# A twelve-part decoder on one core: when the split operands are made, which engine evacuates, and where masks, biases and one-hots are made

## The chip, the core and the metric

The kernel runs on one core of a Trainium2 chip. The metric is the device time of one execution in microseconds; the time of a kernel is the median of several runs. The profile is of one further execution, and its own time is given beside it. Engines are called PE (TensorE, with PEld for its weight loads), DVE (VectorE), ACT (ScalarE), POOL (GpSimd) and SP (SyncE, which only issues DMAs here).

## What is computed

A pre-norm decoder of four layers works on x, 4 batches of 256 rows of 128 numbers, in fp32. Each layer adds three things to x, each computed from a layer norm of x: a self attention, a cross attention to a context of 4 x 512 x 128, and a feed-forward part.

```python
x = x + L0_attn(norm(x))      # 16 heads of 8, with biases
x = x + L0_xattn(norm(x), ctx, key padding mask)
x = x + L0_ffn(norm(x))       # shared expert + 1 of 32 routed experts
x = x + L1_attn(norm(x))      # causal, scores clipped to +-10
x = x + L1_xattn(norm(x), ctx)        # strided keys
x = x + L1_ffn(norm(x))       # 2 of 8 experts
x = x + L2_attn(norm(x))      # linear attention
x = x + L2_xattn(ctx, mask, norm(x))  # 16 heads of 64, keys: ctx and latents
x = x + L2_ffn(norm(x))       # 2 of 8 experts, with biases
x = x + L3_attn(norm(x), causal mask) # low rank
x = x + L3_xattn(norm(x), ctx, ctx, full mask)
x = x + L3_ffn(norm(x))       # ternary weights, quantised activations
```

In an attention, `out = softmax(q k^T) v`, then `out @ Wo + bo`. The weights of one softmax sum to one, so a bias on v comes out as `bv @ Wo`, the same for every row.

## The kernel before

x stays in SBUF as eight tiles of 128 rows; batch b has tiles 2b and 2b+1. The stages follow one another: layer 0 (self and cross attention together, about 0 to 272 us of the span), its experts (to 328), layer 1's attentions (to 466) and experts (to 558), linear attention (to 631), latent attention (to 1068), its experts (to 1163), and layer 3 (to the end).

**Units and slots.** In layers 0, 1 and 3, `woven` (L432) works on units: one batch of one attention. Layers 0 and 3 have eight, four of self attention and four of cross attention (`self_units` L888 or `low_rank_units` L935, and `cross_units` L910). A unit needs a pass over its rows, which only finds each row's maximum (`rows_of` L546, read by DVE in L571 or, with an additive mask, in L575), and a pass over its columns, which makes the scores again in transposed form, less the maxima, and exponentiates them on ACT (`columns_of` L635, L673). Then `weighted` (L695, L701) multiplies with the values, and the result is divided (L719, L721), transposed, projected and added to x (L740). Slot n weaves, beat by beat, the columns of unit n with the rows of units n+1 and n+2; a beat is two groups of tiles (`beat` L756, `beats` L774). Only the last beats of a slot touch rows of unit n+2. At the end of a slot the maxima of unit n+1 are split in three bf16 parts (`parts` L599), transposed (`parts_T` L614: L629, or L620 and an addition in L626 for split units), and its columns can begin.

Everything that has to be done in a slot is a pair of a position between 0 and 1 and a function; `run` (L849) sorts them and issues them. In layers 0 and 3 this order is the order of the instructions on DVE, ACT, PE and POOL (`manual_schedule`, L857 to L859), each of which takes its own in order. `front` (L811) places the prelude of unit n+2 (norm, source, for cross units key source, then queries and keys), the values of unit n+1 (0.6), and the list `beside`; `back` (L829) places the beats and what follows them.

**Split units.** From the third unit on (`u.split`, L854), the queries and keys of layers 0 and 3 are split in three bf16 parts on POOL (`in_parts` L467, L471 to L474), written to DRAM by three DMAs each (L496, L520), and read back in the layout that the row scores need (L497, L526). All these DMAs are issued by SP, in order. Row scores are then L582, column scores L679. Three sets of buffers rotate.

**Norms.** `statistics` (L300) has its sums on DVE (L308, L309), the power on POOL (L314, L316) and the scaling (L322) on POOL where `on=G`. `turned` (L883) transposes a pair of tiles on PE (L332) and moves it out of PSUM with `evacuate` (L288), which alternates between DVE (L292) and ACT (L294).

**Between stages.** The experts' results lie in DRAM. `bring` (L1373) gathers a batch of them with indirect DMAs on POOL (L1379: two per batch after layer 0, four after layers 1 and 2), `add` (L1386) adds them to x. They are kept in `unsettled`; `settle` (L1219), called from a unit's norm, keeps two batches fetched and adds one. In the expert stages `blocks_of` (L1122) turns expert choices into blocks of rows: ranks, one-hots of ranks (L1136), block numbers, and at last `token` (L1197), which the first gather (L1284) waits for.

**Masks.** `key_mask` (L373) loads a mask and turns it into numbers on DVE (L387); the latent stage calls it at its start (L1879). `added_mask` (L2267) does it for layer 3, whose four masks are made at the stage's start (L2326, L2327). In layer 3 a mask is added to the row scores by DVE while it takes their maximum (L575) and to the column scores by a product with the identity on PE (L643).

Of the kernel before, what the change touches and what calls it, by code (L numbers as in the profile page):

```python
# [101 lines left out]
def _layout(i):  # L102
# [31 lines left out]
        _col(bq[:128][byd]), _col(bq[128:256][byd]),  # L134
# [4 lines left out]
        _col(f["L0_xattn_q_b"][byd]), _col(bk[:128][byd]),  # L139
# [13 lines left out]
        _col(f[k + "bq"][byd]), _col(f[k + "bk"][byd]),  # L153
# [50 lines left out]
def decoder(ctx: ExitStack, tc: tile.TileContext, dr, out):  # L204
# [81 lines left out]
    turn = [0]  # L286

    def evacuate(dst, src):  # L288

        turn[0] ^= 1  # L290
        if turn[0]:
            V.tensor_copy(dst, src)  # L292
        else:
            A.copy(dst, src)  # L294
# [106 lines left out]
    class Unit:  # L401
# [7 lines left out]
        def __init__(u, b, nk, weights, prelude, context, q_bias=None, k_bias=None, v_bias=None,  # L409
                     rows_mask=None, row_mask=None, cols_mask=None, key_bias=None, clip=False):  # L410
            u.b, u.nk, u.weights, u.prelude, u.context = b, nk, weights, prelude, context
            u.q_bias, u.k_bias, u.v_bias = q_bias, k_bias, v_bias
# [19 lines left out]
    def woven(pool, units, n_keys, split=None, lent=None):  # L432
# [95 lines left out]
        def values(u):  # L528
# [10 lines left out]
            if u.v_bias is None:  # L539
                V.tensor_copy(dst, src)  # L540
            else:
                bias = u.v_bias.rearrange("p (h d) -> p h d", h=H)
                for i in range(u.nkt):
                    V.tensor_tensor(dst[:, i], src[:, i], bias, ALU.add)

        def rows_of(u, qt, g, half):  # L546
# [6 lines left out]
            def made(j, r):  # L553
# [9 lines left out]
                def score(i, r=r, sc=sc):  # L563
                    T.matmul(
                        sc[:, i, :], lhsT=u.qm[r, g + i, qt * P : (qt + 1) * P], rhs=u.kc[r, :],
                        start=u.row_mask is None, stop=True,
                    )

                def read(j=j, sc=sc):
                    if u.rows_mask is None:  # L570
                        V.tensor_reduce(u.mx[:, qt, j, g : g + per], sc, AX.X, ALU.max)  # L571
                        return
# [23 lines left out]
                return [], rounds, read  # L596
# [214 lines left out]
        def front(n):  # L811
# [3 lines left out]
            if n + 2 < len(units):  # L815
                u = units[n + 2]
                if u.split:
                    end = 0.35 if units[n].nk < SK else 0.5
                    out += spread(prelude(u)[1 if n else 0 :], 0.0, end)
                else:  # L820
                    out += spread(prelude(u), 0.0, 0.95 - lead)
            if split and n + 3 < len(units):
                out += [(0.8, prelude(units[n + 3])[0])]
# [31 lines left out]
        halves_of_rows = [halved(groups_of_rows(u)) for u in units]  # L855

        by_hand = {mybir.EngineType.DVE, mybir.EngineType.Activation, mybir.EngineType.PE}  # L857
        by_hand.add(mybir.EngineType.Pool)
        with tc.manual_schedule(engines=by_hand) if split else nullcontext():  # L859
# [3 lines left out]
            if len(units) > 1:  # L863
                first += spread(prelude(units[1]), 0.0, 0.8)
            first += beats([], halves_of_rows[0] + halves_of_rows[1][:LEAD], units[0])[0]
# [10 lines left out]
            run(carried)  # L876

# [9 lines left out]

    def self_units(pool, w, biased, clip, first_row):  # L888
        q_bias = scaled(pool, w[:, 512:513]) if biased else None

        def norm(u):
            settle()
            u.xn = normalised(u.b, pool, on=G)

        def source(u):
            u.source = u.key_source = turned(u.xn, pool)
            if biased:
                add_bias(2 * u.b, first_row + 1)
                add_bias(2 * u.b + 1, first_row + 1)

        return [
# [3 lines left out]
                **dict(q_bias=q_bias, k_bias=w[:, 513:514], v_bias=row(first_row)) if biased else {},  # L905
            )
            for b in range(B)
        ]

    def cross_units(pool, w, first_row, context, **masks):  # L910
# [5 lines left out]
        def source(u):  # L916
            u.source = turned(u.xn, pool)
            add_bias(2 * u.b, first_row + 1)
            add_bias(2 * u.b + 1, first_row + 1)

        def key_source(u):
# [3 lines left out]
        return [  # L925
# [3 lines left out]
                q_bias=q_bias, k_bias=w[:, 513:514], v_bias=row(first_row),  # L929
# [3 lines left out]
        ]  # L933

    def low_rank_units(pool, w, **masks):  # L935
        up = w[:, 192:448]

        def norm(u):
            settle()
# [57 lines left out]
    class Router:  # L997
# [3 lines left out]
        def __init__(r, pool, name, n_e, k, per, gate, probs=False, scored=False, xnT=None):  # L1001
# [9 lines left out]
            r.rank = kept("rank", [P, r.n])  # L1011
            r.sent = dram.tile([NT * P, D], F32, tag=name + "sent", name="sent")

        def steps(r, pool, b, tag):
# [105 lines left out]
            return out + [ranks]  # L1120

    def blocks_of(pool, r, size, widths):  # L1122
# [5 lines left out]

        def in_block(which):

            w = small.tile([P, 16], I32, tag="wi", name="wi", bufs=1)[:, :n]
            V.tensor_scalar(w, which, P - 1, None, ALU.bitwise_and)
            wb = small.tile([P, 16], BF16, tag="wb", name="wb", bufs=1)[:, :n]
            V.tensor_copy(wb, w)
            place = pool.tile([P, n, P], BF16, tag="place", name="place", bufs=1)
            V.tensor_tensor(  # L1136
                place, iotab.unsqueeze(1).to_broadcast([P, n, P]),
                wb.unsqueeze(2).to_broadcast([P, n, P]), ALU.is_equal,
            )
            return place  # L1140
# [19 lines left out]
        if per == P:  # L1160
            ranks = small.tile([P, 16], I32, tag="ranks", name="ranks", bufs=1)[:, :n]
            V.tensor_copy(ranks, r.rank)
            place = in_block(ranks)
# [8 lines left out]
        if per < P:  # L1172
            place = in_block(index)
# [15 lines left out]
        V.tensor_scalar(block[:, 1], block[:, 1], partition, None, ALU.mult)  # L1189
        fill(3, "g")  # L1190
# [28 lines left out]
    def settle():  # L1219

        while unsettled and len(fetched) < 2:
            fetch, add = unsettled.pop(0)
            fetched.append(call(add, fetch()))
        if fetched:
            fetched.pop(0)()

    def mixture(pool, r, weights, wh, wd, activate, biases=None):
# [158 lines left out]
        def add(brought):  # L1386
            for t, i, back in brought:
                if weights is None:
# [477 lines left out]
    def latent_attention(wkv, wqo, router):  # L1866
# [9 lines left out]
        with ExitStack() as st:  # L1876
            st.enter_context(psum_pool("ps2x"))
            pool = attn_pool(st, "l2x")
            neg1, neg1T = key_mask(pool, "mbf1", True)  # L1879
# [372 lines left out]
    def normalise_context(b, i):  # L2252
        for t in (NKT * b + i, NKT * b + i + 1):
            V.tensor_scalar(
# [22 lines left out]
    def layer_0(wh, router):  # L2277
        with ExitStack() as st:
# [7 lines left out]
            def loads():  # L2286
                for i in range(0, 16, 4):
                    cols = slice(i * 512, (i + 4) * 512)
                    tc.keep_in_program_order(A.dma_start(wh[:, cols], dr["e0h"][:, cols]))

            units = self_units(pool, w0a, True, False, 0)
            units += cross_units(
# [4 lines left out]
            for u in units[:B]:  # L2297
# [88 lines left out]
```

## Time and profile before

| | us |
|---|---|
| median of 3 runs | 1498.5 (1496.29 to 1503.18) |
| the profiled execution's own time | 1496.84 |
| its span, first to last instruction | 1495.0 |
| PE, DVE, ACT, POOL busy | 1280.2, 827.9, 723.0, 324.1 |
| mean granted clock of PE | 0.915 |
| PE busy in layer 0's slots (34 to 240) | 180.5 of 206 |
| PE busy in layer 3's slots (1196 to 1435) | 216.2 of 239 |
| exponentials of columns (L673), ACT | 384 of 598 ns |
| maxima of 512 columns (L571), DVE | 192 of 684 ns |

A row of the groups names the line, engine, tile written and tiles read. A row of the waits says who waited for whom, in total, how often and at most. A row of the windows gives the stretch, its length, the busy time of PE, PEld, DVE, ACT and POOL with their instructions, then the granted clock of PE (1.00 is full speed), the DMA engines' share and GB/s. The chain goes back from the last instruction to whatever released each step; its pieces are start, length and line.

### The profile page before, as it was taken

The page shows a single profiled execution, that of the slowest core. Times are in us where ns is not written, and L with a number is a line of the kernel's source. Part 1 is how long each engine was busy: PE and PEld are TensorE (multiplying, and loading weights), DVE is VectorE, ACT ScalarE, POOL GpSimd, SP SyncE. Part 2 cuts the span into 40 slices and gives each one's busy share as a digit, 9 for nine tenths or more (in the row PEclk, how much of TensorE's full clock was granted, in tenths as well). Part 3 has the DMA queues.
Part 4 walks back from the last instruction along what each step waited for, and adds up shares of the span by engine and source line. Part 5 has one row for each costly group of instructions (what it writes and reads, how often), then busy time and mean ns, then how long its engine had stood idle before and what let it go on. Part 6 is the DMA issues. An engine that isn't in the chain of part 4 may idle for free.

```text
span 1495.0 us, 29472 instructions
## 1 busy us (share of the span) xinstructions
PE 1280.2 (86%) x11199; PEld 702.3 (47%) x11200; DVE 827.9 (55%) x2696; ACT 723.0 (48%) x1462; POOL 324.1 (22%) x481
## 2 busy tenths in 40 slices
PE   4879998796787998879999999999689389899984
PEld 2434454353354664535555565554456244444442
DVE  6568884585555446555445444543323466777743
ACT  1434667285542334357766756766212024445563
POOL 4332220344123316000000000000141542323000
PEclk8889999896897999999999999999889569999997
DMA  3531220520232116230110000000311211322000
GB/s 139 195 108 63 64 67 20 232 55 11 85 138 90 40 34 212 77 128 15 57 43 20 27 5 1 1 4 1 117 39 40 59 57 51 110 64 77 6 5 8
DMA packets 50873, 95.85 MB, mean 64 GB/s; under 512 B 6881, under 2 KB 31947, under 8 KB 49067
## 3 DMA queue, kind: packets, MB, share of 16 engines
q1 hardware_dynamic: 45742, 73.42, 14.4%
q10 hardware_dynamic: 1728, 13.86, 2.3%
q0 software_dynamic: 3264, 6.69, 2.1%
q8 instruction: 90, 1.47, 0.4%
q14 instruction: 49, 0.40, 0.1%
HBM read 66.20 MB, written 29.72 MB: 64 GB/s over the span
## 4 chain that ended last, share of the span: by engine, by line
PE 63%; DVE 12%; ACT 7%; POOL 7%; issue 5%; DMA 5%; SPq 1%; ACTq 0%; POOLq 0%; DVEq 0%
PE o L2047 6%; PE g L1306 6%; PE o L701 6%; PE s L2027 5%; PE f L1973 4%; PE s L582 4%; PE y L1330 3%; PE s L679 3%; DVE mx L571 2%; PE s L643 2%; PE f L1959 2%; PE s L364 2%; PE s L656 2%; POOL back L1379 2%; PE t L1315 2%
## 5 line engine op out<-in xcount | busy, mean ns | idle before, releaser
L673 ACT ACTIVATE pr<-s 128x512 f32<-128x512 f32 x384 | 206.1, 598 | 228.6 <-PE s L679 152.0
L314 POOL TENSOR_SCALAR ve<-mv 128x2 f32<-128x2 f32 x44 | 10.1, 230 | 739.4 <-DVE mv L309 739.2
L1984 ACT ACTIVATE ss<-ss,ntop 128x768 f32<-128x768 f32 x128 | 118.6, 928 | 91.8 <-DVE ntop L1982 91.6
L701 PE MATMUL o<-pr,v 128*32 128x256 f32 (+1 forms) x1792 | 145.8, 400 | 9.1 <-ACT os L707 5.5
L571 DVE TENSOR_REDUCE mx<-s 128x1 f32<-128x512 f32 (+1 forms) x192 | 122.5, 684 | 50.1 <-PE s L679 22.4
L1978 DVE CUSTOM_DVE_ANT_0 ss<-f,n 128x512 f32<-128x512 f32 x128 | 83.5, 688 | 69.2 <-PE f L1973 69.2
L2047 PE MATMUL o<-pr,v 128*64 128x256 f32 x768 | 109.4, 397 | 1.0 <-ACT pr L2034 0.9
L575 DVE CUSTOM_DVE_ANT_0 junk<-s,nmif 128x512 bf16<-128x512 f32 x128 | 82.8, 686 | 35.3 <-PE s L679 34.6
L2027 PE MATMUL s<-qT,kT 64*128 64x256 f32 x768 | 101.1, 382 | 0.0
L2034 ACT ACTIVATE pr<-s,n 128x512 f32<-128x512 f32 x128 | 80.3, 679 | 30.0 <-PE s L2027 29.8
L582 PE MATMUL s<-e0h 32*128 32x512 bf16 (+1 forms) x576 | 72.3, 361 | 15.8 <-DMA e0h<-kp 15.2
L1284 POOL DMA_INDIRECT xb<-sent,token x62 | 59.8, 965 | 103.5 <-PE t L1291 58.4
L1973 PE MATMUL f<-kT,qT 64*128 64x512 f32 x256 | 77.1, 629 | 2.2 <-ACT kT L294 1.1
L1966 DVE CUSTOM_DVE_ANT_0 ss<-f,nought 128x256 f32<-128x256 f32 x128 | 46.7, 421 | 54.8 <-PE f L1959 51.8
L2047 PEld LDWEIGHTS o<-pr,v 128*64 128x64 f32 x768 | 48.4, 137 | 58.6 <-issue 25.9
L701 PEld LDWEIGHTS o<-pr,v 128*32 128x32 f32 x1792 | 39.0, 110 | 71.2 <-issue 48.6
L2027 PEld LDWEIGHTS s<-qT,kT 64*128 64x128 f32 x768 | 67.8, 191 | 6.2
L679 PE MATMUL s<-e0h 32*128 32x256 bf16 x960 | 68.4, 276 | 2.5 <-DVE mx L571 1.7
L332 PE MATMUL s<-consts,xn 128*128 128x128 f32 x64 | 20.3, 369 | 54.7 <-POOL xn L322 54.7
L575 DVE CUSTOM_DVE_ANT_0 junk<-s,nmcau 128x256 bf16<-128x256 f32 x128 | 46.2, 420 | 28.1 <-PE s L656 12.0
L656 PE MATMUL s<-qm,kc 32*128 32x512 f32 (+1 forms) x256 | 60.0, 676 | 0.0
L322 POOL TENSOR_SCALAR xn<-x,mv,rs 128x128 f32<-128x128 f32 x72 | 57.7, 809 | 3.8
(482 smaller groups left out, 2643.9 us busy)
## 6 DMA issues: line engine op xcount, KB each, us to landing
qp<-qp SPq DMA_DIRECT2D x36, 192.0 KB, 2.3
kd<-ahead SPq DMA_DIRECT2D x20, 256.0 KB, 2.0
vd<-ahead SPq DMA_DIRECT2D x20, 256.0 KB
kT<-kd SPq DMA_DIRECT2D x20, 256.0 KB, 4.8
v<-vd SPq DMA_DIRECT2D x5, 1024.0 KB, 5.3
e0h<-qp SPq DMA_DIRECT2D x6, 768.0 KB
e0h<-in_e0h ACTq DMA_DIRECT2D x4, 1024.0 KB, 7.2
e0h<-in_e0h SPq DMA_DIRECT2D x1, 4096.0 KB
```

The source lines that it names most:

```text
L571: V.tensor_reduce(u.mx[:, qt, j, g : g + per], sc, AX.X, ALU.max)
L575: V.tensor_tensor_reduce(junk[:, : u.nk], sc[:, i, :], u.rows_mask(qt), 1.0, -3e38, ALU.add, ALU.max, accum_out=u.mx[:, qt, j, g + i : g + ...
L582: T.matmul(sc[:, i, :], lhsT=u.q3[r, g + i, c, qt * P : (qt + 1) * P], rhs=u.kk[r, g + i, : u.nk], start=n == 0, stop=n == 3 * per - 1,)
L656: T.matmul(sc, lhsT=u.kc[r, kt * P : (kt + 1) * P], rhs=u.qm[r, gp : gp + 2, first:], start=u.clip, stop=True,)
L673: A.activation(dst, sc, AF.Exp)
L679: T.matmul(sc[:, i, :], lhsT=u.kk[r, gp + i, kt * P : (kt + 1) * P], rhs=u.q3[r, gp + i, c, :], start=u.cols_mask is None and n == 0, stop ...
L701: T.matmul(u.po[gp][32 * j : 32 * j + 32, i, first:], lhsT=u.v[:, kt, 4 * j + gp + i, :], rhs=u.pr[gp, kt, j][:, i, first:], start=kt + i ...
L1306: T.matmul(p[r], lhsT=xbT[b][:, r], rhs=w(512 * i), start=biases is None, stop=True,)
L1973: T.matmul(sc[h], lhsT=qT[u, c][hrow[h], qt * P : (qt + 1) * P], rhs=kT[u, c][hrow[h], :SK], start=True, stop=True,)
L1984: A.activation(ss[qt][h], ss[qt][h], AF.Exp, bias=ntop[:, qt, h, c : c + 1], accum_out=total[:, qt, h, c : c + 1],)
L2027: T.matmul(sc[h][:, i, :], lhsT=kT[u, c][hrow[h], kt * P : (kt + 1) * P], rhs=qT[u, c][hrow[h], :], start=False, stop=i == 1,)
L2047: T.matmul(po[u, g][hrow[h], i, :], lhsT=v[u][:, kt, n * hd : (n + 1) * hd], rhs=pr[u, g, kt, h][:, i, :], start=kt + i == 0, stop=kt + i ...
```

## The change

- **Preludes.** For a split unit n+2, queries and keys go to 0.06 and 0.12 of slot n. What comes ahead of them is done in slot n-1: norm at 0.68, source (and key source) between 0.8 and 1.0. For the third unit the norm is at 0.85 of the opening and the source at 0.02 of slot 0.
- **`reducing`.** While layers 0 and 3 are woven, `evacuate` and the values' copy always use ACT.
- **Biases.** The value bias is multiplied with the output weights once (`output_bias`) and added to x with the output bias, by POOL, beside the unit's slot.
- **First units.** The first unit of layers 1 and 3 fetches only its own batch, adds and normalises tile by tile, with the scaling on DVE, and fetches the second batch then (`settled_LN`). The first unit of layer 3 gets its row mask by a product on PE.
- **Masks and context.** The latent stage's mask is made ahead of the linear attention. Layer 3's full masks are made beside units 1 and 2. Layer 0's context is normalised on POOL (L2254). The first half of the routed weights is loaded one quarter a slot in slots 0 to 3.
- **One-hots.** The last router makes the one-hots of ranks batch by batch; three of four are made in the latent stage.

```diff
     def evacuate(dst, src):
         turn[0] ^= 1
-        if turn[0]:
+        if turn[0] and not reducing:
             V.tensor_copy(dst, src)
         else:
             A.copy(dst, src)
...
-            if u.v_bias is None:
+            if reducing:
+                A.copy(dst, src)
+            else:
                 V.tensor_copy(dst, src)
-            else:
-                bias = u.v_bias.rearrange("p (h d) -> p h d", h=H)
-                for i in range(u.nkt):
-                    V.tensor_tensor(dst[:, i], src[:, i], bias, ALU.add)
...
+                by_product = u.rows_mask is not None and u.n == 0
+
+                def masks():
+                    T.matmul(
+                        sc, lhsT=identb,
+                        rhs=u.rows_mask(qt).unsqueeze(1).to_broadcast([P, per, u.nk]),
+                        start=True, stop=False,
+                    )
                 def read(j=j, sc=sc):
-                    if u.rows_mask is None:
+                    if u.rows_mask is None or by_product:
                         V.tensor_reduce(u.mx[:, qt, j, g : g + per], sc, AX.X, ALU.max)
                         return
...
                 if u.split:
-                    end = 0.35 if units[n].nk < SK else 0.5
-                    out += spread(prelude(u)[1 if n else 0 :], 0.0, end)
+                    steps = prelude(u)
+                    out += [(0.06, steps[-2]), (0.12, steps[-1])]
+                    if n == 0:
+                        out += [(0.02, steps[1])]
                 else:
                     out += spread(prelude(u), 0.0, 0.95 - lead)
             if split and n + 3 < len(units):
-                out += [(0.8, prelude(units[n + 3])[0])]
+                steps = prelude(units[n + 3])
+                out += [(0.68, steps[0])] + spread(steps[1:-2], 0.8, 1.0)
...
+            if split:
+                first += [(0.85, prelude(units[2])[0])]
...
+    def output_bias(pool, w, n):
+        made = []
+        def make():
+            t = pool.tile([P, S], F32, tag="q", name="q")[:, :P]
+            V.tensor_copy(t, w[:, 514:515].to_broadcast([P, P]))
+            acc = product(t, w[:, 384:512], "s1")
+            made.append(pool.tile([P, P], F32, tag=f"ob{n}", name=f"ob{n}", bufs=1))
+            V.tensor_tensor(made[0], acc, row(n), ALU.add)
+        def add(u):
+            for t in (2 * u.b, 2 * u.b + 1):
+                G.tensor_tensor(x[t], x[t], made[0], ALU.add)
+        return make, add
...
+    def to_one_hots(place, which):
+        n = which.shape[1]
+        w = small.tile([P, 16], I32, tag="wi", name="wi", bufs=2)[:, :n]
+        if which.dtype != I32:
+            V.tensor_copy(w, which)
+            which = w
+        V.tensor_scalar(w, which, P - 1, None, ALU.bitwise_and)
+        wb = small.tile([P, 16], BF16, tag="wb", name="wb", bufs=2)[:, :n]
+        V.tensor_copy(wb, w)
+        V.tensor_tensor(
+            place, iotab.unsqueeze(1).to_broadcast([P, n, P]),
+            wb.unsqueeze(2).to_broadcast([P, n, P]), ALU.is_equal,
+        )
...
-        while unsettled and len(fetched) < 2:
+        while len(fetched) < 2 and unsettled:
+            bring_next()
+        if fetched:
+            fetched.pop(0)()
+
+    def bring_next():
+        if unsettled:
             fetch, add = unsettled.pop(0)
             fetched.append(call(add, fetch()))
-        if fetched:
-            fetched.pop(0)()
+
+    def settled_LN(b, pool):
+        if not fetched:
+            bring_next()
+        add = fetched.pop(0)
+        xn = []
+        for t in (2 * b, 2 * b + 1):
+            add(t)
+            n = pool.tile([P, D], F32, tag="xn", name="xn", bufs=5)
+            normalise([x[t]], [n])
+            xn.append(n)
+        bring_next()
+        return xn
...
-            V.tensor_scalar(
+            G.tensor_scalar(
                 cn[:, t, :], cn[:, t, :], context_mv[:, t, 0:1], context_rs[:, t : t + 1],
...
-            mf, mfT = added_mask(pool, "mif1", 2, False), added_mask(pool, "mif1T", NKT, False)
...
+            units[1].beside += [make, call(full_mask, "mif1", 2)]
+            units[2].beside += [call(full_mask, "mif1T", NKT)]
...
+    with tc.tile_pool(name="late2", bufs=1, reuse_waits="tile") as late2:
+        latent_mask = key_mask(late2, "mbf1", True)
```

The hunks that only pass these things on are left out.

## The prediction, written before the result was known

> **What bounds the kernel now.** The page's shares come first, then its slices, then the chain of work that ended last, the table of waits for TensorE, and the timeline around the longest waits.
>
> ```profile
> PE 1280.2 (86%) x11199; PEld 702.3 (47%) x11200; DVE 827.9 (55%) x2696; ACT 723.0 (48%) x1462; POOL 324.1 (22%) x481
> ...
> PEclk8889999896897999999999999999889569999997
> ...
> PE 63%; DVE 12%; ACT 7%; POOL 7%; issue 5%; DMA 5%; SPq 1%; ACTq 0%; POOLq 0%; DVEq 0%
> ```
>
> TensorE is busy 86% of the span, but only 63% of the chain; the rest is handovers, and its clock sags at the start, around the middle of layer 0 and at the start of layer 3. The change leaves TensorE's work as it is, so what it can win is waits, and the slow clock after them. The waits of TensorE in layer 0 (34 to 250 us) and layer 3 (1200 to 1300 us), as "who waited for whom: us, times, longest":
>
> ```profile
> PE s L582 <- DMA e0h<-kp: 15.2, 4, 5.5
> PE s L620 <- DVE mp L612: 2.3, 3, 1.3
> PE s L650 <- DVE mT L292: 1.7, 1, 1.7
> ...
> PE s L582 <- DMA cn<-kp: 3.8, 1, 3.8
> PE s L582 <- DMA kk<-kp: 2.3, 1, 2.3
> PE s L332 <- POOL xn L322: 2.1, 2, 1.8
> ```
>
> The row scores (L582) wait six times, 21.2 us, for operands that go out to DRAM and back. One such trip in the chain of waits, unit 3 of layer 0:
>
> ```profile
> 65.15 0.48 ACT q L491
> ...
> 68.68 1.92 SPq L496
> ...
> 72.65 1.92 DMA kp<-kp
> ...
> 74.58 5.57 DMA e0h<-kp
> ...
> 80.29 0.37 PE s L582
> ```
>
> From the query copy to the first matmul it takes 15.1 us; the others 13.6 (unit 2), 14.1 (unit 4), in layer 3 12.4 and 15.0. After each wait the granted clock (third number from the end) is near a half for 5 to 7 us:
>
> ```profile
> 56.00:60.00 4.00, 4.00 (x38) 1.60 (x34) 2.01 (x6) 1.09 (x2) 0.31 (x1) 0.55 0.46 162
> 80.00:88.00 8.00, 7.71 (x69) 3.82 (x70) 2.91 (x7) 1.71 (x4) 4.37 (x7) 0.57 0.16 66
> 106.00:112.00 6.00, 5.65 (x67) 3.20 (x68) 2.96 (x7) 1.49 (x3) 2.43 (x5) 0.60 0.02 4
> 1232.00:1238.00 6.00, 6.00 (x47) 2.21 (x44) 2.01 (x12) 1.49 (x4) 2.26 (x3) 0.57 0.01 4
> ```
>
> **The change part by part**, against the profiled execution's own 1496.84 us (span 1495.0).
>
> **1. Operands a slot ahead (-16.5).** A slot lasts from one transpose of the row maxima (L629, L620) to the next: 26.0, 25.3, 25.2, 30.0, 33.7, 32.4, 33.9 us in layer 0. Unit n+2's queries and keys sit at about 0.17 and 0.29 of slot n (0.19 and 0.44 in cross slots); they go to 0.06 and 0.12. Its rows are first read after six of eight beats, 0.75 of a self slot. Without its wait and half its slow clock a self slot lasts some 20 us, so rows are wanted 15 us after its start, and the trip ends at 1.2 + 13.6 to 15.1 = 14.8 to 16.3. I leave 4.7 us of the 21.2 in place. SP's queue carries the same DMAs; the 4 MB of e0h on ScalarE's queue go out 1 MB a slot instead of all in slot 0. Ends: -21 and -5.
>
> **2. The clock after those waits (-7.5).** About 29 us run at half speed behind five of them; were TensorE alone the limit, 14.5 would go. A beat there is some 2.0 us with 2 x 684 ns of VectorE in it, so I take half. [...]
>
> **3. A new wait on the transposes (+8).** The norm moves from 0.8 to 0.68 of the slot, but the transpose (L332) that needs it moves from early in the next slot to 0.8 to 1.0 of the same one. The nearest trace of that:
>
> ```profile
> 1208.67 0.29 DVE L308 BATCH_NORM_STATS2 st<-x 128x6 f32<-128x128 f32 x1
> ...
> 1210.82 1.57 POOL L322 TENSOR_SCALAR xn<-x,mv,rs 128x128 f32<-128x128 f32 x2
> ...
> 1211.68 0.47 PE L332 MATMUL s<-consts,xn 128*128 128x128 f32 x1 [1.84 <-POOL xn L322]
> ```
>
> Statistics to xn take 3.7 us, and VectorE runs behind its place (in slot 4 the statistics of 0.8, due at 164.7, come at 167.87: 3.2 us). The room is 0.17 x 20 = 3.4 us in self slots (0.22 for a self unit: 4.4), 0.17 x 33 = 5.6 in cross ones. With a lag of 1 us in self and 2.5 in cross slots, the five slots lose 0.3 + 1.3 + 1.3 + 0.6 + 0.6 = 4.1, twice 8.2. Behind the waiting transpose stand all of TensorE's later beats. Ends: 0 and +25.
>
> **4. Less on VectorE (-6).** In a cross slot of layer 0 it loses four bias adds (4 x 283 ns, L544), four context normalisations (4 x 338, L2254) and half its evacuations (0.95): 3.4 us of 25 to 27 busy. Layer 3 loses 1.5. At each slot's end VectorE is last (chain of 165 to 172: half is L571), yet mid-slot TensorE leads. I pass on 0.4 of it in slots 3 to 6 of layer 0 (5.4) and 0.2 in layer 3's (1.2). Ends: 0 and -15. ScalarE takes the copies (about 1.5 us a slot; busy 20 of 32): covered, but not in the last slots, where only exponentials run: +1.2. GpSimd takes the 16 normalisations. [...] The folded value biases cost one product and two copies a layer: under 1 us, beside the first slots.
>
> **5. First units (-7.5).** At layer 3's start GpSimd issues eight gathers (1.25 us each) from 1163.78, and ve starts at 1173.61. With four they end at 1168.8; tile 1's sums land at 1170.2, then 0.5 statistics, 1.1 ve and rs, 0.34 on VectorE: 1172.8 instead of 1176.4. The other four gathers go where GpSimd waits for q (1176.4 to 1180.7); after qm, four more and the norm, unit 1's xn comes about 3 us sooner. Unit 2's norm in the opening removes the 1.84 + 0.30 + 0.46 at 1211.68 (2.6), mT on ScalarE rather than behind VectorE's reads 0.8 here and 1.7 at 33.8. Layer 1: two gathers more before unit 1, +0.5 (-1.5 to +1.5).
>
> **6. Masks.** The latent stage opens with VectorE idle 5.0 us for mrow (L387), then 1.4 of work; keys wait behind it and L1959 starts at 640.68. Without it, some 637, where the key loads land too: -3.5, less 0.3 if the mask's DMA is late in the stage before. In layer 3 the two full masks become 512 KB loads behind a bounce on SP, read by VectorE at 0.83 and 0.75 of slots 1 and 2; if the load is not there VectorE stands, and with it the reads that free PSUM: +2 (0 to +5). Masks by product: 16 reads of 0.61 us (L571's pace) for 32 of 0.345, -1.3 on VectorE, against 16 matmuls like L643's (0.5 us at half clock) on a TensorE 12 of 33 us busy: 0 (-1.3 to +3).
>
> **7. One-hots (-1.3).** At ffn2's start L1136's 2.29 us and three casts leave the token chain, about 1.0 of it stays. Nothing, if xb does wait for line<-part, as the chain has it.
>
> Sum: -16.5 - 7.5 + 8 - 6 + 1.2 - 7.5 - 3.2 + 2 - 1.3 = -30.8, so 1466.0; the median shown is 1.66 above the profiled time, so 1467.7: **1468**.
>
> **Rivals.**
> - **All of it works:** -21, -12, part 3 at +3, VectorE -9, rest as above: -48, **1451**. For it: TensorE has no other wait over 2 us in those slots. 0.12.
> - **The trip still decides:** a slot that shrinks also brings the need forward, and 13.6 to 15.1 us are wanted out of some 15. Part 1 gives 8, part 2 gives 2: +14, **1482**. 0.13.
> - **Nothing measurable:** part 3 eats parts 1 and 2 (+16 more, and VectorE's relief not passed on, +6, masks +3): **1493**. The change then doesn't do what it says. 0.09.
> - **Slower:** TensorE, in order, stands at L332 for GpSimd's xn. Price: 3.7 + 3.2 of lag + 0.8 for a normalisation in front, less 3.4 to 5.6 of room, 2 to 4 us, and a half-clock stretch of 3 us: 6.5 in ten slots, 65 instead of 8, **1525**. It decides from 3.9 us a slot, where the 38.8 of the other parts are gone. Against it: the lag shrinks with VectorE's load. 0.08.
> - The forecast: 0.58.
>
> **How the numbers follow.** Range 1443 to 1492: it leaves out most of the slower case and some of the best and the unmeasurable one. Faster by over 0.5% (about what a measurement can tell from no change; under 1491): 0.58 + 0.12 + 0.13 = 0.83; within: 0.09; slower: 0.08.
>
> **What would show it.** Right: L582 waits for its DMA under 6 us in all; no half-clock stretch after 60 us in layer 0's self slots; unit 0's second xn of layer 3 near 1173 less what was won before; no DVE wait on mrow. Wrong: L332 waiting for xn over 10 us in all, VectorE idle for mi in layer 3, ACT rows ending the last slots later.

## The result, and the profile after

The changed kernel takes **1475.0 us** (median of 4 runs, 1473.1 to 1481.2) beside 1498.1 for the one before (one run more than above): ratio 0.985, 95% interval 0.983 to 0.988. That is 23 us faster; 30 were forecast. The profiled execution spans 1472.6 us. Its page, in the rows that answer to those of before (engine sums, granted clock in 40 slices, the chain by engine):

```profile
PE 1267.6 (86%) x11222; PEld 698.2 (47%) x11222; DVE 810.2 (55%) x2586; ACT 738.5 (50%) x1502; POOL 335.1 (23%) x497
...
PEclk8979999896897999999999999999889679999997
...
PE 68%; DVE 12%; ACT 7%; POOL 4%; issue 4%; DMA 3%; SPq 0%; ACTq 0%; POOLq 0%; DVEq 0%
```

TensorE's share of the chain rose from 63 to 68%: DMA and GpSimd gave up five points. TensorE's waits in layer 0 (34 to 250 us), then at the start of layer 3 (1183 to 1290):

```profile
PE s L591 <- DMA e0h<-kp: 13.3, 3, 9.7
...
PE s L333 <- POOL xn L323: 2.8, 2, 2.5
```

```profile
PE s L333 <- POOL xn L323: 4.2, 2, 3.9
```

L591 (L582 before) still waits 13.3 us in layer 0, now mostly in one wait of 9.7; in layer 3 its DMA waits are gone. Among the slots, L333 (L332) waits for xn at one place in each layer, the start of slot 0.

By stage, from the same marks in both traces (transposes of maxima, first gathers, first latent row scores):

| stretch | before | after | difference | by the prediction's steps |
|---|---|---|---|---|
| start to layer 0's last slot | 237.8 | 231.4 | -6.4 | about -20 |
| to ffn0's gather, to layer 1's gather | 95.0 | 93.8 | -1.2 | 0 |
| layer 1, to ffn1's gather | 145.9 | 149.7 | +3.8 | +0.5 |
| to the linear attention; to the first latent rows | 162.0 | 157.2 | -4.8 | -3.2 |
| latent stage, to ffn2's gather | 444.6 | 437.0 | -7.6 | -1.3 |
| ffn2, to layer 3's gather | 78.5 | 78.4 | -0.1 | 0 |
| layer 3 | 331.3 | 325.2 | -6.1 | about -7.6 |

So the total is right partly by luck, because misses cancel: layer 0 gave 13 us less than forecast and layer 1 3 less, the latent stage with its opening 8 more. One profile's stretch is uncertain by up to some 4 us: three of the runs below (e0h's loads in the cross slots; the same with layer 1's gathers ahead; that with the one-hots at ffn2's start) have the same code up to layer 1, and took 95.6, 99.3 and 95.3 us for the second row. The clock differs from execution to execution: the four runs of the changed kernel were granted 0.922 to 0.931 of full speed, and the slowest had the lowest.

The 9.7 us wait, in SyncE's timeline, in the DMA engines' share (the number before the last) while SyncE stands, and in the chain of waits of the changed kernel:

```profile
62.89 1.85 SPq L521 DMA_DIRECT2D kp<-kp  x3
64.80 0.49 SPq L523 DMA_DIRECT2D kp<-n  x1
75.58 0.33 SPq L498 DMA_DIRECT2D e0h<-qp  x1
```

```profile
66.00:70.00 4.00, 4.00 (x64) 2.21 (x56) 3.16 (x8) 2.05 (x5) 1.24 (x2) 1.00 0.04 8
```

```profile
70.59 0.06 ACT pr L683
70.65 4.92 DMA e0h<-in_e0h
...
75.58 0.33 SPq L498
...
76.02 4.70 DMA e0h<-kp
...
80.85 0.37 PE s L591
```

SyncE has issued the last leg of unit 3's operands to DRAM by 65.3, but it issues the read-back (L498) only at 75.58, in the instant in which an unrelated 1 MB load of e0h, issued by ScalarE at 70.65, has landed. From 66 to 70 the DMA engines were 4% busy, so it was not their bandwidth that it lacked. The semaphores in the trace say why. The 266 DMAs of SyncE and ScalarE in it use eight, 101 to 108, 33 or 34 times each, and the next DMA in time takes the next of them in 263 of 265 steps. The other two are here: L497 at 60.50 passes over 101, and the load and L498 both take it.

```
SyncE    60.50 to 64.80  3 qp<-qp, 3 kp<-kp, 1 kp<-n  raise 102 to 108
SyncE    65.34, 65.39    (L498, unit 3)               waits for 103, for 104 and 102: three of its legs
ScalarE  70.65           e0h<-in_e0h (load of slot 1) raises 101 sixteen times, from 74.87 to 75.57
SyncE    75.58           e0h<-qp (L498, unit 3)       waits for 101, raises 101
```

The load stands ahead of the legs in the program, but ScalarE, whose order is written by hand, reaches it 10 us after SyncE began the legs (60.50).

### The profile page after: what moved, and what is told of

Its sections match the earlier page's. It is cut to its first block, busy times and chain, and to the rows that moved or that the text cites. A ratio compares the mean times of both kernels' runs of the same rounds, so it can differ in the third digit from the quotient of the medians.

```text
span 1472.6 us, 29442 instructions
## 1 busy us (share of the span) xinstructions
PE 1267.6 (86%) x11222; PEld 698.2 (47%) x11222; DVE 810.2 (55%) x2586; ACT 738.5 (50%) x1502; POOL 335.1 (23%) x497
## 4 chain that ended last, share of the span: by engine, by line
PE 68%; DVE 12%; ACT 7%; POOL 4%; issue 4%; DMA 3%; SPq 0%; ACTq 0%; POOLq 0%; DVEq 0%
PE o L711 6%; PE o L2131 6%; PE g L1388 6%; PE s L2111 5%; PE s L591 4%; PE f L2057 4%; PE s L689 3%; PE y L1412 3%; PE s L653 3%; DVE mx L580 3%; PE s L365 2%; PE s L666 2%; PE f L2043 2%; PE s L2104 2%; PE t L1397 2%
## 5 line engine op out<-in xcount | busy, mean ns | idle before, releaser
L683 ACT ACTIVATE pr<-s 128x512 f32<-128x512 f32 x384 | 206.1, 599 | 180.6 <-PE s L689 128.6
L315 POOL TENSOR_SCALAR ve<-mv 128x2 f32<-128x2 f32 (+1 forms) x46 | 10.6, 231 | 740.1 <-DVE mv L310 739.9
L580 DVE TENSOR_REDUCE mx<-s 128x1 f32<-128x512 f32 (+1 forms) x208 | 132.0, 683 | 64.8 <-PE s L689 24.5
L591 PE MATMUL s<-e0h 32*128 32x512 bf16 (+1 forms) x576 | 69.3, 350 | 13.9 <-DMA e0h<-kp 13.3
L333 PE MATMUL s<-consts,xn 128*128 128x128 f32 x64 | 20.7, 370 | 58.0 <-POOL xn L323 40.2
L666 PE MATMUL s<-qm,kc 32*128 32x512 f32 (+1 forms) x256 | 57.5, 662 | 0.0
L1461 POOL DMA_INDIRECT back<-done,index x40 | 39.6, 991 | 52.2 <-DMA done<-ys 33.8
```

Of the source, the lines that this page charges most:

```text
L591: T.matmul(sc[:, i, :], lhsT=u.q3[r, g + i, c, qt * P : (qt + 1) * P], rhs=u.kk[r, g + i, : u.nk], start=n == 0, stop=n == 3 * per - 1,)
L666: T.matmul(sc, lhsT=u.kc[r, kt * P : (kt + 1) * P], rhs=u.qm[r, gp : gp + 2, first:], start=u.clip, stop=True,)
L683: A.activation(dst, sc, AF.Exp)
```

## Experiments

Ratios, with their 95% intervals, are to the kernel before in runs on the same chip. The first four kernels ran on one chip, the next four on a second, the last four on a third; between these groups the ratios are compared, not the medians.

**Loads in slot 0 again** (1483.3 us; 0.990, 0.987 to 0.993).

```diff
-                u.beside += [call(context_scales, u.b), call(loads, u.b)]
+                u.beside += [call(context_scales, u.b)]
+            units[0].beside += [call(loads, i) for i in range(4)]
```

> The changed kernel, with the four 1 MB loads of e0h all issued in slot 0 again, instead of one per slot. Theory (turn of the semaphores): in the changed kernel's program the read-back of unit 3's queries (L498) is given the same DMA completion semaphore as the e0h load that stands eight transfers ahead of it, so it can't be issued before that load has landed; that is the 9.72 us wait at 80.85. With the loads in slot 0 they have landed by then: the L591 wait of slot 1 falls to 2 us or less, slot 1 from 29.7 to some 22 us, and the whole to 1465 to 1469. Rival (crowding): the wait comes of the loads sharing the DMA engines with the operands' legs; then moving them into slot 0 only moves it to slots 0 and 1, L591 keeps 8 us or more of waits in layer 0, and the time stays at 1473 to 1477.

Slot 1 fell from 29.7 to 21.1 us as the first theory has it, but slot 0 rose from 22.1 to 34.7 with a wait of 12.8, so the time missed both. SyncE's timeline, and ScalarE's:

```profile
42.66 12.07 SPq L521 DMA_DIRECT2D kp<-kp  x3
58.46 0.29 SPq L523 DMA_DIRECT2D kp<-n  x1
```

```profile
49.21 0.38 ACTq L2372 DMA_DIRECT2D e0h<-in_e0h  x1
...
51.01 0.33 ACTq L2372 DMA_DIRECT2D e0h<-in_e0h  x1
```

Three key legs, 1.9 us elsewhere, last 12.1, to 54.73. A load took 5.0 us to land in this run, which puts the landing of the one of 49.21 at 54.2, when the third leg begins if it is as long as elsewhere (0.55 us); and the burst of transfers that the loads are part of, from 50.0 on, is over at about 58, just ahead of L523 at 58.46. From 45.2 to 50.0 the DMA engines were 2% busy, so crowding doesn't explain the wait of the third leg in that time; the turn of the semaphores, seen in the changed kernel's trace, would explain both waits. That the third leg waits for the first load and L523 for the second is thus the author's estimate from these times. Four loads in slot 0 are not harmful in themselves: before, they were issued together, from 57.5 to 59.4, between two units' legs.

**Loads in the cross slots** (1471.7; 0.981, 0.979 to 0.983).

```diff
-                u.beside += [call(context_scales, u.b), call(loads, u.b)]
+                u.beside += [call(context_scales, u.b)]
...
                 u.beside += [call(normalise_context, u.b, i) for i in range(0, NKT, 2)]
+                u.beside += [call(loads, u.b)]
```

> The changed kernel, with the four loads of e0h one each in the cross slots 4 to 7, where no row score of the self slots waits. Both theories (turn of the semaphores, crowding) expect slot 1's wait at L591 to fall from 9.7 us to under 2 and the time to 1464 to 1469. They differ beside the run with the loads in slot 0: by the turn of the semaphores the two are within 2 us of each other, by crowding this one is 6 us or more the faster. If neither holds (SP's own order, or GpSimd's splits, decide), slot 1 stays at 28 us or more in both.

Slot 1 took 19.9 us without a DMA wait, as expected, though the time came down by only 3.3 (by the ratios 6.6, and the two intervals just overlap), less than expected: this profile lost 5 us more than the changed kernel's to the slow clock in slot 0. It was 12 us faster than the run with the loads in slot 0, which crowding had foretold in size; but by the estimate above that run's loss was the semaphores' too.

**Row masks in VectorE's reads** (1478.1; 0.987, 0.984 to 0.990).

```diff
-                by_product = u.rows_mask is not None and u.n == 0
+                by_product = False
```

> The changed kernel, with the row masks of layer 3's first unit not made by product on TensorE, but in VectorE's read of each head as before. Theory (the product lies on the path): TensorE has the 16 mask products (0.455 us each) ahead of scores that VectorE is already waiting for, so from unit 1's normalised rows to the first transpose of maxima the changed kernel takes 14.1 us against 12.1 before; undone, layer 3's first transpose comes 2 us earlier and the time is 1473. Rival (VectorE is relieved): single reads cost VectorE 2.5 us more, so the time is 1476 to 1478.

In layer 3's opening the first transpose of maxima came 37.5 us after the first gather instead of 39.6, so the products are on the path there, but the time shows no gain; slots 0 to 2 of layer 3 took 80.8 us instead of 78.1, as the rival has it. Of the changed kernel's chain of waits:

```profile
1161.41 1.82 PE s L572 x4
1163.23 2.06 PE s L563 x16
1165.29 4.87 DVE mx L580 x8
```

Mask products and scores follow each other on TensorE while VectorE has nothing to read. The last experiment below bears on the sum.

**Layer 1's first unit as before** (1477.6; 0.986, 0.984 to 0.988).

```diff
-            if u.b == 0 and unsettled:
-                u.xn = settled_LN(0, pool)
-                return
```

> The changed kernel, with layer 1's first unit normalised as before (two units' sums fetched ahead, both tiles normalised on GpSimd); layer 3 keeps the new way. Theory (the fetch of unit 1 comes late): in the changed kernel unit 1's gathers are issued only after unit 0's rs, 335.1 instead of about 329, though GpSimd was idle for 5.6 us before; undone, unit 1's xn comes 2 us earlier and unit 3's up to 4.7, layer 1's lost 3.8 us come back, and the time is 1471. Rival (the layer was lost elsewhere, TensorE's order): the time stays within 1 us of 1475.

Layer 1 took 147.1 us instead of 149.7, 2.6 of the 3.8; the time shows nothing of it. The mechanism is shown better by the run that only fetches earlier (below).

**Operands not ahead, loads in the cross slots** (1486.5; 0.990, 0.987 to 0.993).

```diff
-                    steps = prelude(u)
-                    out += [(0.06, steps[-2]), (0.12, steps[-1])]
-                    if n == 0:
-                        out += [(0.02, steps[1])]
+                    end = 0.35 if units[n].nk < SK else 0.5
+                    out += spread(prelude(u)[1 if n else 0 :], 0.0, end)
...
-                steps = prelude(units[n + 3])
-                out += [(0.68, steps[0])] + spread(steps[1:-2], 0.8, 1.0)
+                out += [(0.8, prelude(units[n + 3])[0])]
...
-                first += [(0.85, prelude(units[2])[0])]
```

> The changed kernel with e0h's loads in the cross slots, and the operands not a slot ahead: queries, keys and their source at the old places (the source at the start of the slot, 0 to 0.35 or 0.5; the norm at 0.8), unit 2's norm not in the opening. It stands beside the run with the same loads and the operands ahead (1471.7). By the prediction's steps 1 to 3 the placement is worth 16.5 + 7.5 - 8 = 16: 1488. By the profiles (slots 0 to 2 of layer 0 add up to 76.5 us before and 67.9 with the loads out of the way, those of layer 3 to 80.0 and 78.0) it is worth about 10: 1482, with L591 waiting 12 us or more for its DMA in layer 0 again. Rival (the gain comes of fewer copies on VectorE, not of the placement): 1474 or less.

The hunk of the loads, as above, is left out. L591 waits for its DMAs in layer 0 and in layer 3 again:

```profile
PE s L591 <- DMA e0h<-kp: 11.3, 4, 4.4
...
PE s L591 <- DMA cn<-kp: 3.5, 1, 3.5
```

The placement is worth 14.8 us by the medians, 13 by the ratios, whose intervals are apart: steps 1 to 3 had 16 together.

**The kernel before, loads in the cross slots** (1497.5; 0.999, 0.996 to 1.001).

```diff
-            units[0].beside += [loads]
...
+                u.beside += [call(loads, u.b)]
```

> The kernel before, with e0h's four loads one each in the cross slots 4 to 7. Before, ScalarE issues all four between 57.5 and 59.4, after unit 2's legs are through and 9 us ahead of unit 3's. Theory (there they are in nobody's way, and the change's own spreading put them in the way): the time stays within 2 us of before, the 13.6 to 15.1 us trip and its waits at L582 stay. Rival (the loads are what the trips of before wait for): L582's waits in layer 0 fall from 15.2 us to under 8, and the time by 6 to 10.

No change in the time. In the profile L582 kept 11.2 of its 15.2 us in layer 0:

```profile
PE s L582 <- DMA e0h<-kp: 11.2, 3, 5.5
```

What went is unit 3's wait at 80.3 us, 3.5 long. Slot 1 took 21.8 us instead of 25.3, and the last slot began at 233.1 instead of 237.8; but the stretch to layer 1's gather took 98.9 instead of 95.0. So the loads were in the way of one trip before, and cost nothing that the time shows.

**The kernel before, with the latent mask made early** (1486.2; 0.991, 0.988 to 0.994).

```diff
-            neg1, neg1T = key_mask(pool, "mbf1", True)
+            neg1, neg1T = latent_mask
...
+        latent_mask = key_mask(late2, "mbf1", True)
```

> The kernel before, with one edit of the change: the latent stage's key mask is made ahead of the linear attention, in a pool of its own. The changed kernel gained 4.9 us up to the first latent row scores, and 7.6 more from there to ffn2's first gather. Theory A (the edit gives the opening only): about 3.2 us by the prediction, up to 5 by the profile: 1493 to 1495. Theory B (it gives the stage's inner gain too, since the stage's order of work is made by the planner from what waits for what): 10 us or more, 1486 to 1489.

The stretch to the first latent rows fell from 77.8 to 73.2, that behind it from 444.6 to 442.0. So the edit gives some 4.6 us at the opening (3.2 forecast) and not the inner 7.6. The 4.6 is rough: over all profiles the stretch is 72.7 to 77.0 in the twelve kernels with the early mask, 77.8 and 79.8 in the two without. The time, 13.6 us lower by the ratio, within 4.3, agrees with theory B's figure, but 3.6 us of this profile's 10.8 lie in stages that the edit can't reach: the verdict is by the stretches.

**Loads in the cross slots and layer 1's gathers ahead** (1468.8; 0.979, 0.976 to 0.983).

```diff
-                u.xn = settled_LN(0, pool)
+                u.xn = settled_LN(0, pool, 2)
...
-        if not fetched:
+        while len(fetched) < ahead and unsettled:
...
```

> The changed kernel with e0h's loads in the cross slots, and in layer 1 (not in layer 3) the second unit's gathers issued ahead of the first unit's norm, while GpSimd is idle. Against the run with the loads alone (1471.7): by the theory of the late fetch, unit 1's xn of layer 1 comes 3 us earlier than in the changed kernel and the layer's loss of 3.8 us goes: 1468. Rival (layer 1 is bound elsewhere): 1471 to 1472.

GpSimd in layer 1, in the changed kernel (first gather 325.21) and in this run (first gather 323.62):

```profile
326.49 1.04 POOL L1461 DMA_INDIRECT back<-done,index  x1 [0.30 <-issue]
...
335.08 1.09 POOL L1461 DMA_INDIRECT back<-done,index  x1 [0.17 <-issue]
...
341.88 1.59 POOL L323 TENSOR_SCALAR xn<-x,mv,rs 128x128 f32<-128x128 f32 x2
```

```profile
326.25 0.94 POOL L1461 DMA_INDIRECT back<-done,index  x1 [0.30 <-issue]
...
338.35 1.59 POOL L323 TENSOR_SCALAR xn<-x,mv,rs 128x128 f32<-128x128 f32 x2
```

Unit 1's normalisation starts 14.7 us after the first gather instead of 16.7 (before: 14.7), unit 3's 22.8 instead of 27.4; the layer takes 148.4 us. Over all profiles layer 1 takes 149.3 to 151.1 us in the five kernels with the late fetch and 145.3 to 148.5 in the nine without, with nothing between. So the theory holds for the layer; its size in the time, 3 us, is inside the intervals.

**The same, one-hots all at ffn2's start** (1470.3; 0.983, 0.980 to 0.985).

```diff
-            router = Router(late, "r2", 8, 2, P, gates[:, 40:48], probs=True, places=late2)
+            router = Router(late, "r2", 8, 2, P, gates[:, 40:48], probs=True)
```

> The run with e0h's loads in the cross slots and layer 1's gathers ahead (1468.8), with the one-hots of the latent stage's ranks made all at once at ffn2's start again, instead of batch by batch in the stage. The prediction's step 7 put the edit at 1.3 us, at ffn2's start: then the stretch from the first latent row scores to ffn2's first gather goes from 436.3 to about 437.6. The changed kernel gained 7.6 us in that stretch, of which moving the mask alone showed 2.6. Theory (the batch-wise one-hots change the planner's order and give the other 5): the stretch is 441 or more, the time 1473 or more. Rival (they give the 1.3 alone): 1470.

The stretch took 441.9 us instead of 436.3, which is the theory's size; that the planner's order is the reason is not shown. Over all profiles it is 435.2 to 437.8 with the batch-wise one-hots and 441.9 to 444.6 without, with nothing between. The time, 5 us longer by the ratios, agrees, but the intervals overlap. Some 1.6 of the stretch's 5.6 is the start of ffn2 (15.8 against 17.4 from the end of the last projection to the gather), the rest lies inside the stage, where one wait comes and goes with the edit, near 1000 us:

```profile
PE f L2013 <- ACT xnT L295: 1.9, 1, 1.9
```

**The same, copies on VectorE and ScalarE in turn** (1466.0; 0.979, 0.977 to 0.982).

```diff
-        reducing[:] = [1] if split else []
+        reducing[:] = []
```

> The run with e0h's loads in the cross slots and layer 1's gathers ahead (1468.8), with the evacuations of layers 0 and 3 taking turns between VectorE and ScalarE again, and the value copies on VectorE. By the prediction's step 4 less work on VectorE is worth 6.6 us in layer 0's cross slots and layer 3, of which the copies are nearly a half: +3, 1472, seen in slots 3 to 6 of layer 0 (123.4 us in that run). Rival (TensorE leads in those slots, and what they gained was clock): those slots stay within 1 us once the lost clock is taken off, and the time within 1 us of 1469, or lower, since ScalarE is relieved in the last slots.

No difference in the time. Slots 3 to 6 of layer 0 took 128.6 us against 126.5 (not the 123.4 of the expectation); with the lost clock (one minus the granted clock, times the stretch: 4.0 and 3.3) taken off, 124.5 against 123.2. The rival holds, if by 1.3 us instead of 1; the run with the one-hots at ffn2's start, whose layer 0 has the same code as the 123.2, has about 122: moving the copies off VectorE is not what made those slots shorter.

**Unit 2's norm earlier in the opening** (1456.6; 0.973, 0.971 to 0.976).

```diff
-                first += [(0.85, prelude(units[2])[0])]
+                first += [(0.55, prelude(units[2])[0])]
```

> The run with e0h's loads in the cross slots and layer 1's gathers ahead (1468.8), with the norm of unit 2 at 0.55 of the opening instead of 0.85, in layers 0 and 3. In the changed kernel its statistics stand on VectorE behind the opening's last row reads and the split of the maxima (31.23 to 31.95; 1188.19 to 1189.08), so TensorE waits for xn at the first transpose of slot 0: 2.55 + 0.30 in layer 0, 3.89 + 0.30 in layer 3, and the half clock of slot 0 (8.5 us lost in it) follows that. Theory: both waits fall under 1 us, the trip of unit 2 starts 3 us earlier, and the time is 1461 to 1464. Rival (the row reads that the statistics now stand before become late): the first transposes of maxima come 1 us later and the time is 1467 to 1469.

VectorE and TensorE at the end of layer 0's opening, in the changed kernel and in this run:

```profile
25.55 4.88 DVE L580 TENSOR_REDUCE mx<-s 128x2 f32<-128x512 f32 x8 [2.55 <-PE s L563]
...
31.23 0.29 DVE L309 BATCH_NORM_STATS2 st<-x 128x6 f32<-128x128 f32 x1
```

```profile
34.20 0.47 PE L333 MATMUL s<-consts,xn 128*128 128x128 f32 x1 [2.55 <-POOL xn L323]
```

```profile
28.12 0.28 DVE L309 BATCH_NORM_STATS2 st<-x 128x6 f32<-128x128 f32 x1
```

```profile
32.51 0.64 PE L333 MATMUL s<-consts,xn 128*128 128x128 f32 x2
```

The waits at L333 for xn are gone from both layers' slot 0, slot 0 takes 20.1 us instead of 25.8 in layer 0, 23.9 instead of 28.2 in layer 3, and the time falls beyond what was expected. Layer 3's first transpose comes 1.4 us later from its gather, as the rival has it (layer 0's at 32.3 us instead of 30.7), which is little beside that. About 4 of this profile's 16 us lie between layer 0 and layer 3, where the edit can't reach; the time, 9 us by the ratios, is the better measure. Its TensorE waits in layer 0 begin with:

```profile
PE s L591 <- DMA e0h<-kp: 3.3, 2, 2.8
```

This version is faster than both kernels: 2.7% below the one before, and its interval doesn't touch that of any run without the edit.

**The same, masks in VectorE's reads** (1460.9; 0.978, 0.975 to 0.980).

> As the run with the norm of unit 2 at 0.55 of the opening, and the row masks of layer 3's first unit in VectorE's reads instead of by product on TensorE. The run without the products had layer 3's first transpose 2.0 us earlier from its first gather, and no gain in its time (1478.1 beside 1475.0, within its spread). Theory (the products lie on the path in the opening, and the rest of that run was clock): 2 us less than the run with the norm at 0.55. Rival (VectorE's longer reads are paid back in slots 0 to 2): the same or 1 us more.

The first transpose comes 1.2 us earlier from the gather, slot 0 takes 1.3 longer, and the time is 4 us longer, not shorter (the intervals just touch): the rival. The masks by product at least pay for themselves.

## Why the prediction was right, and where it was off

1. **Operands ahead** (-16.5, its clock -7.5, the new wait +8). Their sum, 16, was nearly right: 13 to 15 us, once the loads were out of the way. The step that failed is the clause "the 4 MB of e0h on ScalarE's queue go out 1 MB a slot instead of all in slot 0", costed at nothing: it put a transfer that ScalarE issues late in front of SyncE's read-back. L591 kept 13.3 us instead of 4.7, so the sign "L582 waits for its DMA under 6 us in all" failed. Undoing that alone gave 3 to 7 us.
2. **The clock.** One minus the mean granted clock, times the span: 0.085 x 1495.0 = 127 us lost before, 0.073 x 1472.6 = 107.5 after. In layer 0's slots it fell from 20.4 to 13.7, in layer 3 from 42.8 to 35.8. Not all of this is time, as some of it lies inside waits; what part is, no run separates. But half speed still follows waits in the self slots after 60 us (0.50 at 80 to 84, 0.60 at 106 to 112), so the sign "no half-clock stretch" failed together with step 1. After which waits half speed came, and how long it stayed, is in the last section.
3. **The new wait on the transposes.** It did not come in slots 1 to 7, where 0.68 to 0.8 of a slot was enough for GpSimd; it came at slot 0, 2.8 and 4.2 us, which the prediction had not priced, because there the statistics of unit 2 stand on VectorE behind the opening's last row reads. So +8 was near in size (7.0 of waiting) by luck, and wrong in place; taking the waits away was worth 9 us by the ratios, the clock behind them included.
4. **Less on VectorE** (-6; its parts, 5.4 and 1.2, make 6.6). The copies, a good part of it, give nothing that can be measured. The other parts, bias adds and context normalisations, were not tried alone; what slots 3 to 6 gained from 130.0 to 124.9 is 0.7 us once their lost clock (6.6, then 2.2) is taken off. The +1.2 for ScalarE in the last slots did not come: the last slot's exponentials end 23.0 us after its start in layer 0 (23.6 before), 30.8 in layer 3 (30.8 before).
5. **First units** (-7.5). Tile by tile in layer 3 unit 0's second xn ends 9.3 us after the first gather instead of 12.6, 3.3 sooner (3.6 forecast), and unit 1's norm begins 3.0 sooner (3 forecast). But the first transpose of maxima comes only 1.0 sooner (39.6 instead of 40.5), as the products of step 6 take 2 of it. The waits for mT (1.7 and 0.8) are gone. The 2.6 of unit 2's norm didn't come: the 1.84 + 0.30 + 0.46 of before became 3.89 + 0.30 + 0.46 in slot 0. Layer 1 lost 3.8 instead of 0.5: its second gathers now wait for the first norm, though GpSimd stood idle 5.6 us before it.
6. **Masks.** Latent opening 4.6 to 4.9 instead of 3.2, and VectorE's wait for mrow is gone. Layer 3's full masks, +2 in the forecast, cost VectorE no wait: it reads their loads at 1242.5 and 1257.4 without one. Its one wait for mi, 2.5 us for the causal mask at 1147.2, lies ahead of the first gathered rows (1151.0). By product: 0 forecast; 2 lost in the opening and given back later.
7. **One-hots** (-1.3). The start of ffn2 gave 1.6; the mis-sized term is what the edit does to the stage itself, another 4 us, which no row of before shows. The planner orders that stage from what waits for what, so a changed order is the likely cause; that is argued, not shown. Of the 4 us, one wait of 1.9 at xnT is seen to come and go; the rest, and why, is left open.

So the forecast was right in sign and in its main cause. It was 7 us short: missing were what the loads held up (step 1), the gain of unit 2's norm, in whose place slot 0 got a wait (steps 3 and 5), and layer 1's fetch (step 5). Steps 6 and 7 gave more than forecast, and that they made up for most of it was luck.

## What to carry to other kernels

When a change moves a DMA, count not only its bandwidth and its own queue: look in the trace for the semaphores that it raises and waits for. Here a load that ScalarE issued late held SyncE's read-back from 65.4 to 75.58, as both used semaphore 101. A step moved ahead has to be moved ahead on every engine that it uses: unit 2's norm stood before its transposes in the list, and still behind 2.5 us of row reads on VectorE. And set stretch against stretch before trusting a total: here a gain 13 us short in one stage and 8 over in another hid in a forecast that looked 7 us off.

## What the runs showed of the hardware

The clock record of the profiles has a plain form. In each of the fourteen, every stretch of half speed but the one that the end of the span cuts off lasts 3.41 us or a whole multiple of it, and all of them begin on one grid of that step (in the profiles of the kernel before and the changed one, to 0.012 us). On this grid, the end of the opening and slot 0 of the changed kernel, then of the run with the loads in the cross slots alone (TensorE's busy time is the first number behind the comma, the granted clock the third from the end):

```profile
28.94:32.35 3.41, 1.76 (x18) 0.83 (x14) 3.21 (x12) 0.37 (x1) 0.13 (x1) 1.00 0.03 10
32.35:35.76 3.41, 0.95 (x2) 0.36 (x2) 2.15 (x4) 0.28 (x1) 2.38 (x4) 0.50 0.00 0
35.76:39.18 3.42, 3.27 (x18) 1.77 (x18) 0.01 (x1) 0.57 (x2) 1.26 (x3) 0.50 0.00 0
39.18:42.59 3.41, 2.02 (x23) 1.37 (x24) 1.70 (x4) 1.56 (x3) 1.25 (x3) 1.00 0.31 113
```

```profile
30.31:33.73 3.42, 0.83 (x8) 0.26 (x3) 3.21 (x12) 0.37 (x1) 0.94 (x2) 1.00 0.02 5
33.73:37.14 3.41, 1.74 (x4) 0.87 (x4) 1.20 (x3) 0.37 (x1) 1.57 (x2) 0.50 0.00 0
37.14:40.55 3.41, 2.69 (x18) 1.27 (x16) 0.94 (x2) 1.17 (x3) 2.11 (x4) 0.50 0.00 0
40.55:43.96 3.41, 2.78 (x16) 2.07 (x20) 0.77 (x3) 0.86 (x2) 0.53 (x3) 0.50 0.47 175
43.96:47.38 3.42, 3.42 (x24) 1.43 (x18) 1.83 (x3) 1.08 (x2) 2.44 (x5) 0.50 0.20 59
47.38:50.79 3.41, 3.41 (x26) 1.47 (x24) 0.74 (x2) 1.08 (x2) 0.00 (x0) 0.50 0.75 242
50.79:54.20 3.41, 3.41 (x43) 1.73 (x42) 3.22 (x9) 2.44 (x5) 0.00 (x0) 1.00 0.41 139
```

The two run nearly the same code there, and each has one wait of 2.5 us for the same xn, up to 34.2 and 34.6. But half speed lasts two windows (6.8 us) in the first, whose second window was 96% busy, and five (17.1 us) in the other, whose windows were 51, 79 and 82% busy before one was full.

Counted over the fourteen profiles, from 12 us on, by TensorE's busy share of each window (the ends of matmuls are modelled, so the shares are rough): after a full-speed window less than 45% busy, half speed followed in 191 of 193 cases (in the profiles of the kernel before and the changed one: 33 of 33); after one more than 75% busy, in 18 of 4370 (2 of 620). A half-speed window less than 80% busy was followed by another in all 450 cases (68 of 68); one more than 95% busy by full speed in 296 of 361 (42 of 49).

So a wait of 2 to 3 us had no fixed price here: the half speed after the two waits of 2.5 us was 3.4 and 8.5 us of clock in these two slots. In both, the last window at half speed was over 95% busy (96 and 100%). But full speed did not always come after such a window: not in 65 of the 361, of which the window from 43.96 above is one. In the kernel before, a wait of 2.27 us before 1230.63 lies mostly in one window that was 42% busy, and two at half speed followed:

```profile
1226.93:1230.34 3.41, 1.43 (x14) 0.27 (x10) 3.08 (x15) 1.56 (x3) 0.00 (x0) 1.00 0.78 277
1230.34:1233.76 3.42, 3.13 (x26) 1.79 (x26) 1.78 (x9) 0.72 (x2) 1.92 (x4) 0.50 0.03 7
1233.76:1237.17 3.41, 3.41 (x30) 1.20 (x30) 1.33 (x9) 0.63 (x2) 0.60 (x1) 0.50 0.00 0
1237.17:1240.58 3.41, 2.34 (x21) 0.66 (x14) 1.80 (x9) 1.14 (x3) 0.00 (x0) 1.00 0.00 0
```
